# Products of zeros on TensorE, PSUM operands for x and h, and a reordered end in a graph network's layer

## The chip, the cores and the metric

The kernel runs on one core of a Trainium2 chip. The metric is the device time of one execution in microseconds (us), as the median of several runs. A core has five engines that run at the same time and meet through semaphores: TensorE (PE, matrix products, with its weight loads shown apart as PEld), VectorE (DVE), ScalarE (ACT), GpSimd (POOL) and SyncE (SP, which issues most of the DMA transfers). SBUF is the working memory, PSUM the one into which TensorE writes.

## What is computed

12,500 nodes with 128 features each, and 412,500 edges, sorted by target node. In short:

```
h    = relu(layernorm(x)) @ W_in2f                       # 12500 x 128
W_e  = (ssp(edge_attr @ W_f1 + b_f1) @ W_f2 + b_f2) * edge_weight   # 412500 x 128
msg  = h[dst] * W_e
agg  = segment_sum(msg, src, 12500)
out  = x + ssp(agg @ W_o1 + b_o1) @ W_o2 + b_o2          # ssp(v) = softplus(v) - log 2
```

`dst` is sorted, so the rows of `h` that a run of edges reads lie near each other. `src`, over which the messages are summed, is in random order.

## The kernel before

**Chunks.** The edges are taken in 806 chunks (`NCH`) of 512, four tiles of 128 edges each; four chunks make a `Group`. The chunks are split into seven segments (`SEGS`) of 88, 44, 30, 14, 14, 8 and 4 groups. The first ends at chunk 352, the sixth at 792.

**One chunk.** The filter's first layer (`hidden`, L691) is done for two chunks at once, 20 x 512 products into the PSUM tile `z`; ACT takes Abs, Exp and Ln of it (L700 to L703) and DVE puts the softplus together (`hidden_end`, L709). The second layer (`value`, L801) adds four products into a PSUM tile `v` that ACT has filled with the bias (L793). `pick` (L812) chooses the rows of `h` for each edge: DVE marks the place of each edge's target in a window of 32 rows (`at`, L785), and PE multiplies that with the rows, kept as three bf16 parts, into the PSUM tile `picked`; ACT scales them by the edge weight into `hg` (L822). `message` writes `v * hg` into the SBUF tile `o`, of which there are 8 (L829, L830), and POOL scatters `o` with four indirect DMAs (L834) into a table in HBM that has room for several messages of each node. The slot of each message is ranked with two products on PE (`after` and `rest_of`, L733 and L766, into the PSUM tile `free`), and DVE's comparison and maximum (L714, L738). `v` and `picked` share three PSUM buffers. A helper, `behind`, makes some products wait for scatters of some chunks earlier.

**Collecting.** When a segment's messages are in its table, they are loaded back (`load`, L873, into `m`, six buffers), DVE marks which node each belongs to (`compare`, L886, into `to`), and PE sums them per node (`add`, L907, into the PSUM tile `acc`, four blocks of 128 nodes at a time, here called a quad). `keep` then adds `acc` to the running sums `agg` in SBUF (L928 on ACT for the first segment, L930 on DVE for the others). A unit is up to six tiles of one `load`. The units of the first six segments are spread over the steps of later chunks by a small planner. It starts `DELAY` = 7 chunks behind a segment, works out an even rate up to step `NCH + BEYOND`, and then deals the units out to steps; within a step it stops at a unit that ends a quad:

```
        while i < len(todo) and todo[i][0] < k:
            ...
            i += 1
            if todo[i - 1][1].ends(todo[i - 1][2]):
                break
```

**The order.** It is written out by hand (`manual_schedule`): `step(k)` issues, for chunk k, the message; the ends of the ranks before; `keep` of finished quads; for k + 1 the scaling and the second layer; for k + 2 the picking and the bias; then windows, `hidden_end`, the comparison of blocks, `compare` of the step's units, ranks, logarithms, the first layer of a pair four chunks ahead, and `add` of the units (each one unit late). Each engine runs its own part of this in order.

**Making h.** `make_h` does 4 x 128 rows at a time (a quad, 25 in all), one new quad every ninth step: statistics, normalisation, a transpose, Relu, the product `hps` in PSUM, and then three bf16 parts of it. ACT writes the first, DVE subtracts it from `hps` into the SBUF tile `left` (L370), ACT writes the second, DVE subtracts that from `left` for the third (L373).

**The end.** 25 quads of `x` are loaded ahead. The first `NX` = 14 are early ones, from step 300 on, with their bias added by DVE (L426); the others come from step 804 on, into tiles that have come free, with their bias added by POOL. After the last step the last segment is collected, and `finish` applies the output layers to each quad (L436 to L450) and stores it (L453).

Of the kernel before, what the change touches and what calls it, by code (L numbers as in the profile page):

```python
# [17 lines left out]
P = 128  # L18
TG = 16
CH = 512  # L20
# [23 lines left out]
def gnn_kernel(  # L44
# [282 lines left out]
    def make_h(q, psum):  # L327

        n = min(QT, NTILE - q * QT)
        xb = early.pop(q, None)  # L330
        if xb is None:
            xb = load_x(q)
            for _ in range(3):
                yield
        st = ln.tile([P, QT, 6], F32, name="st")
        mv = ln.tile([P, QT, 2], F32, name="mv")
        for i in range(n):
            nc.vector.bn_stats(st[:, i, :], xb[:, i, :])
            nc.vector.bn_aggr(mv[:, i, :], st[:, i, :])

        rs = ln.tile([P, QT], F32, name="rs")
        nc.scalar.activation(rs[:, :n], mv[:, :n, 1], AF.Ln, bias=eps)
        nc.scalar.activation(rs[:, :n], rs[:, :n], AF.Exp, scale=-0.5)
        yield

        ve = ln.tile([P, QT], F32, name="ve")
        nc.vector.tensor_scalar(ve[:, :n], mv[:, :n, 1], EPS, -0.5, op0=ALU.add, op1=ALU.mult)
        r2 = ln.tile([P, QT], F32, name="r2")
        nc.vector.tensor_mul(r2[:, :n], rs[:, :n], rs[:, :n])
        nc.vector.tensor_mul(r2[:, :n], r2[:, :n], ve[:, :n])  # L350
        nc.vector.scalar_tensor_tensor(rs[:, :n], r2[:, :n], 1.5, rs[:, :n],
                                       op0=ALU.add, op1=ALU.mult)
        for i in range(n):
            nc.vector.tensor_scalar(xb[:, i, :], xb[:, i, :], mv[:, i, 0:1], rs[:, i:i + 1],
                                    op0=ALU.subtract, op1=ALU.mult)
        yield
        xps = psum.tile([P, QT, P], F32, name="xps", tag="acc")
        for i in range(n):
            nc.tensor.transpose(xps[:, i, :], xb[:, i, :], ident)
        xT = ln.tile([P, QT, P], F32, name="xT")  # L360
        nc.scalar.activation(xT[:, :n, :], xps[:, :n, :], AF.Relu)
        yield
        hps = psum.tile([P, QT, P], F32, name="hps", tag="acc")
        for i in range(n):
            nc.tensor.matmul(hps[:, i, :], xT[:, i, :], win, start=True, stop=True)
        hb = ln.tile([P, QT, 3, P], BF16, name="hb")
        nc.scalar.activation(hb[:, :n, 0, :], hps[:, :n, :], AF.Copy)
        yield
        left = ln.tile([P, QT, P], F32, name="left")
        nc.vector.tensor_sub(left[:, :n, :], hps[:, :n, :], hb[:, :n, 0, :])  # L370
        nc.scalar.activation(hb[:, :n, 1, :], left[:, :n, :], AF.Copy)
        yield
        nc.vector.tensor_sub(hb[:, :n, 2, :], left[:, :n, :], hb[:, :n, 1, :])  # L373
        for (b, rows), table in zip(tables, h3_t):
            lo = max(0, b - q * QN) // P
            hi = min(n, (b + rows - q * QN) // P)
            if lo < hi:
                r = q * QN + lo * P - b
                nc.sync.dma_start(
                    table[r:r + (hi - lo) * P, :].rearrange("(c p) f -> p c f", p=P),  # L380
                    hb[:, lo:hi, :, :].rearrange("p c k f -> p c (k f)"))
                if b + rows == QN:
                    yield
            if q == NQ - 1:
                for r in range(NTILE * P - b, rows, P):
                    if r >= 0:
                        nc.sync.dma_start(table[r:r + P, :], none)
        nc.sync.dma_start(
            h3[q * QN:q * QN + n * P, :].rearrange("(c p) f -> p c f", p=P),
            hb[:, :n, :, :].rearrange("p c k f -> p c (k f)"))  # L390
        yield
# [28 lines left out]
        for p, cs, rows in pieces:  # L420
            nc.sync.dma_start(xo[:p, cs, :], x[rows, :].rearrange("(c p) f -> p c f", p=p))

    def x_bias(xo, pieces, engine=nc.vector):
        for p, cs, rows in pieces:
            xi = xo[:p, cs, :]
            engine.tensor_add(xi, xi, spread(bo2[:p, :], xi.shape[1]))  # L426

    def finish(t0, n, sT, quad, psum, z, xo=None, bank=("v", 3)):

# [108 lines left out]
    with tc.tile_pool(name="edge", bufs=2) as edge, tc.tile_pool(  # L538
# [8 lines left out]
        free_v = free.rearrange("p (t b) -> p t b", b=NBLK)  # L547


        count_ps = state_ps.tile([P, P], F32, name="count_ps")  # L550

        def clear(seg):

            todo = []

            def put(b, e, low):

                half = seg.tiles(b) * P // 2
                v = seg.views[VIEWS][seg.row(b):seg.row(e), :].rearrange(
                    "(r c) f -> r (c f)", c=half)  # L560
                for q in range(0, 2 * (e - b), P):
                    n = min(P, 2 * (e - b) - q)
                    for r in range(low, half - low, ZN * ZR):
                        w = min(ZN * ZR, half - low - r)
                        todo.append((
                            v[q:q + n, r * RW:(r + w) * RW].rearrange("r (k f) -> r k f", f=ZR * RW),
                            zero[:n, None, :].to_broadcast([n, w // ZR, ZR * RW])))

            full = (NBLK - 1) // BG * BG
            for b, e in ((0, seg.b0), (seg.b0, min(seg.b1, full)), (seg.b1, full)):  # L570
                if b < e:
                    put(b, e, seg.low)

            for b in range(full, NBLK):
                low = seg.low if b < NBLK - 1 else seg.low_last
                half = seg.tiles(b) * P // 2
                n = (half - 2 * low) // ZR
                for r in range(2):
                    r0 = seg.row(b) + r * half + low
                    todo.append((seg.views[VIEWS][r0:r0 + n * ZR, :]  # L580
                                 .rearrange("(q c) f -> q (c f)", c=ZR), zero[:n, :]))
            return todo

        puts = []

# [8 lines left out]
        class Group:  # L594
# [91 lines left out]
            def hidden(self, c):  # L686

                z = psum.tile([P, 2, CH], F32, name="z")
                for k in range(2):
                    rows = slice(32 * (c + k), 32 * (c + k) + RBF)  # L690
                    mm = nc.tensor.matmul(z[:, k, :], wf1[rows, :], self.f[rows, :],  # L691
                                          start=True, stop=True)
                    if k == 0:
                        behind(mm, self.g * NCHUNK + c - LZ, 3)
                self.pair[c] = z
# [110 lines left out]

            def pick(self, c, at, ps):

                near = self.near.pop(c)
                k = self.g * NCHUNK + c - 2  # L810
                for i in range(QT):
                    mm = nc.tensor.matmul(ps[:, i, :], at[:, i * P:(i + 1) * P], near,  # L812
                                          start=i == 0, stop=i == QT - 1, skip_group_check=True)
                    if i == 0:
                        behind(mm, k, 2 + k % 2)
# [118 lines left out]
        groups = {}  # L934
        NEXT = table_of.index(1) - 1
        LG, LW, LR, LZ = 12, 6, 6, 4
        DELAY, BEYOND = 7, 14

        def of(k):
            return groups[k // NCHUNK], k % NCHUNK  # L940
# [52 lines left out]
        def step(k, units=()):  # L993
# [19 lines left out]
                for _ in r:  # L1013
                    pass
            tops.clear()
            for c in owed:
                c.keep()
            owed.clear()
            if has(k + 1):
                g, c = of(k + 1)  # L1020
                hgs[k + 1] = g.picked(c, ps.pop(k + 1))
# [10 lines left out]
            part("blocks", min(k + LR + 1, 2 * k + 3), blocks)  # L1032
            for c, u in units:
                c.compare(u)
            upto = max(made["rank"], min(k + LR, 2 * k + 3))
            ready = [ranks(j) for j in range(made["rank"] + 1, upto + 1)]
            made["rank"] = upto
# [63 lines left out]
                if todo[i - 1][1].ends(todo[i - 1][2]):  # L1101
                    break

        def x_ahead(homes, engine):

            pending = []
            for q, xo in homes:
# [5 lines left out]
                yield  # L1113
                yield
                if len(pending) > 2:
                    x_bias(*pending.pop(0), engine)
            for w in pending:
                yield
                x_bias(*w, engine)

        def as_quad(t):
            return t.rearrange("p (c f) -> p c f", f=P)

        xs = {}
        NX = 14

        def early_homes():
            for q in range(NX):
                if q < 6:
                    yield q, quad.tile([P, QT, P], F32, name="xo", bufs=6)  # L1130
                elif q < 12:
                    yield q, ln.tile([P, QT, P], F32, name="xo", tag=("xb", "xT", "left")[q // 2 - 3],
                                     bufs=2)
                else:
                    t = ln.tile([P, QT, 3, P], BF16, name="xo", tag="hb", bufs=2)
                    yield q, as_quad(t.rearrange("p c k f -> p (c k f)")[:, :2 * CH].bitcast(F32))
# [14 lines left out]
        def rest():  # L1151
# [14 lines left out]
                    yield  # L1166
            yield from ranges(psum)
            late_biases(psum)

        def side():  # L1170

# [11 lines left out]
        with tc.manual_schedule():  # L1183
# [27 lines left out]
            made["rank"] = 0  # L1211
            group(1)
            aside = side()
            x_early = x_ahead(early_homes(), nc.vector)
            x_late = x_ahead(late_homes(), nc.gpsimd)
            for k in range(-3, max(NCH, max(units) + 1)):
                for seg, d in zeros.get(k, ()):
                    seg.clears.append(nc.sync.dma_start(*d).ins.name)
# [122 lines left out]
```

## Time and profile before

| | |
|---|---|
| median of 6 runs | 4225.73 us (4221.04 to 4228.44) |
| profiled execution: time | 4223.44 us |
| profiled execution: span from the first to the last instruction | 4221.6 us |
| busy PE, PEld | 3356.8 us, 2610.9 us |
| busy DVE, ACT, POOL | 3145.7 us, 2775.0 us, 3142.4 us |
| mean granted TensorE clock | 0.828 of full speed |
| moved by DMA | 820.65 MB, 194 GB/s on average |

All rows are of one execution, taken by the hardware profiler. In its lines "L834" is line 834 of the kernel, "slots<-o" the tile written and the one read (POOL's scatter here), "x3224" the number of such instructions; then busy time in us and the mean ns of one, and behind the bar the idle time of the engine just before these instructions with what ended it. Lines of waits give who waited, for whom, the sum in us, how often, and the longest. Lines of the timeline give start, length, engine, line and operation; neighbours alike are merged. A matmul in fp32 is shown as two instructions. The granted clock is what a throttle leaves of TensorE's full speed.

### The profile page before, as it was taken

To read this page: it belongs to the slowest core of one execution; us is meant where nothing else is said; L and a number is where in the kernel's file an instruction comes from. 1 tells how busy PE (TensorE), PEld (TensorE's weight loads), DVE (VectorE), ACT (ScalarE), POOL (GpSimd) and SP (SyncE) were. 2 spreads that over 40 slices of the span, in tenths; PEclk is the share of its full clock that TensorE was granted. 3 is DMA by queue.
4 is the path that set the end of the run, shared out by engine and by line. 5 is a ranking of instruction groups with operands and counts; after the bars stand their busy time and mean duration, and the time that the engine had idled before them with its cause. 6 is when DMAs were issued, how large, how long until landed. Compare 5 with 4: busy or idle time off the path is not lost. (4 is left out here: it accounts for less than half of the span.)

```text
span 4221.6 us, 74340 instructions
## 1 busy us (share of the span) xinstructions
PE 3356.8 (80%) x21594; PEld 2610.9 (62%) x21594; DVE 3145.7 (75%) x7101; ACT 2775.0 (66%) x5466; POOL 3142.4 (74%) x3292
## 2 busy tenths in 40 slices
PE   6777777667767676688888888888888888988888
PEld 4445444444444444467777777776777776777777
DVE  8767666666555555678878877888888888888887
ACT  7767666676666666666666666666666666666644
POOL 6777777777777777777777777777777777777772
PEclk8767666776666766779999899999999998999999
DMA  6665565555444345467777777778777886887776
GB/s 182 199 193 168 165 191 166 156 170 169 140 115 124 110 134 159 141 204 221 223 220 254 232 209 219 212 213 263 227 211 207 260 247 191 231 247 202 206 210 183
DMA packets 515221, 820.65 MB, mean 194 GB/s; under 512 B 177188, under 2 KB 312728, under 8 KB 514812
## 3 DMA queue, kind: packets, MB, share of 16 engines
q1 hardware_dynamic: 411212, 602.55, 50.2%
q0 software_dynamic: 103168, 213.15, 15.0%
q8 instruction: 180, 2.95, 0.3%
q14 instruction: 229, 1.88, 0.2%
q10 hardware_dynamic: 432, 0.13, 0.0%
HBM read 419.75 MB, written 395.69 MB: 193 GB/s over the span
## 5 line engine op out<-in xcount | busy, mean ns | idle before, releaser
L834 POOL DMA_INDIRECT slots<-o,slot x3224 | 3104.9, 963 | 1003.7 <-issue 757.9
L907 PEld LDWEIGHTS acc<-to,m 128*128 128x128 f32 x8152 | 1069.3, 210 | 245.8 <-issue 137.2
L801 PEld LDWEIGHTS v<-wf,r 128*128 128x128 f32 x6448 | 1009.1, 236 | 249.2 <-issue 171.4
L907 PE MATMUL acc<-to,m 128*128 128x128 f32 x8152 | 1133.6, 298 | 28.6 <-DVE to L886 24.0
L822 ACT ACTIVATE hg<-picked,rcut 128x128 f32<-128x128 f32 x3224 | 911.9, 365 | 309.6 <-PE picked L812 224.0
L801 PE MATMUL v<-wf,r 128*128 128x128 f32 x6448 | 1086.6, 323 | 10.3 <-ACT v L793 8.2
L793 ACT ACTIVATE v<-bf 128x512 f32<-128x512 f32 x806 | 484.9, 602 | 694.2 <-DVE o L830 677.5
L691 PE MATMUL z<-f,wf 20*128 20x512 f32 x1612 | 583.7, 807 | 416.5 <-DVE r L709 408.5
L829 DVE COPY o<-place 128x4 f32<-128x4 f32 x806 | 153.5, 190 | 773.5 <-DMA slots<-o,slot 771.9
L886 DVE TENSOR_TENSOR to<-count_ps,m 128x640 f32<-128x640 f32 (+3 forms) x793 | 630.5, 822 | 37.0 <-PE acc L907 31.5
L812 PE MATMUL picked<-near,at 96*128 96x128 bf16 x3224 | 363.0, 243 | 336.6 <-DVE o L830 315.9
L830 DVE TENSOR_TENSOR o<-v,hg 128x512 f32<-128x512 f32 x806 | 552.9, 686 | 58.0 <-PE v L801 50.4
L709 DVE SCALAR_TENSOR_TENSOR r<-z,nbf,a 128x1024 f32<-128x1024 f32 x403 | 512.8, 1273 | 47.1 <-ACT a L703 46.9
L812 PEld LDWEIGHTS <-at 96*128 96x128 bf16 x3224 | 289.4, 111 | 388.6 <-issue 344.0
L700 ACT ACTIVATE a<-z,bf 128x1024 f32<-128x1024 f32 x403 | 443.7, 1101 | 130.7 <-PE z L691 130.5
L691 PEld LDWEIGHTS z<-f,wf 20*128 20x128 f32 x1612 | 146.3, 221 | 600.0 <-DVE r L709 566.0
L703 ACT ACTIVATE a<-a,half 128x1024 f32<-128x1024 f32 x403 | 462.8, 1148 | 13.1
L738 DVE TENSOR_REDUCE top<-free 128x4 f32<-128x392 f32 x806 | 445.9, 553 | 7.6 <-PE free L733 7.6
L714 DVE TENSOR_TENSOR inb<-count_ps,blk 128x392 f16<-128x392 f32 x806 | 443.6, 551 | 0.0
L701 ACT ACTIVATE a<-a 128x1024 f32<-128x1024 f32 x403 | 426.0, 1057 | 12.8
L766 PE MATMUL free<-inb,rest_of 128*128 128x392 f16 x806 | 306.5, 380 | 48.1 <-DVE top L738 33.8
L733 PE MATMUL free<-inb,after 128*128 128x392 f16 x806 | 308.9, 383 | 6.6 <-DVE inb L714 4.1
(113 smaller groups left out, 1358.7 us busy)
## 6 DMA issues: line engine op xcount, KB each, us to landing
m<-slots SPq DMA_DIRECT2D x307, 387.0 KB
m<-slots SPq DMA_DIRECT2D x278, 322.5 KB
rel<-rel_d SPq DMA_DIRECT2D x202, 384.0 KB
slots<-o,slot POOLq DMA_INDIRECT x3224
m<-slots SPq DMA_DIRECT2D x193, 258.0 KB
slots<-zero SPq DMA_DIRECT2D x96, 387.0 KB
f<-in_f_t SPq DMA_DIRECT2D x404, 80.0 KB
slots<-zero SPq DMA_DIRECT2D x58, 516.0 KB
```

The source lines that it names most:

```text
L691: mm = nc.tensor.matmul(z[:, k, :], wf1[rows, :], self.f[rows, :], start=True, stop=True)
L703: nc.scalar.activation(a, a, AF.Ln, bias=half, scale=0.5)
L709: nc.vector.scalar_tensor_tensor(r, z, nbf1, a, op0=ALU.max, op1=ALU.add)
L738: nc.vector.tensor_reduce(self.top[:, c * QT:(c + 1) * QT], free_v, axis=mybir.AxisListType.X, op=ALU.max)
L793: nc.scalar.activation(v, spread(bf12, QT), AF.Copy)
L801: mm = nc.tensor.matmul(v[:, i, :], r[:, i * P:(i + 1) * P], wf2, start=False, stop=True, skip_group_check=True)
L812: mm = nc.tensor.matmul(ps[:, i, :], at[:, i * P:(i + 1) * P], near, start=i == 0, stop=i == QT - 1, skip_group_check=True)
L822: nc.scalar.activation(hg[:, i, :], ps[:, i, :], AF.Copy, scale=self.rcut[:, j:j + 1])
L830: nc.vector.tensor_mul(o[:, :, :P], v, hg)
L834: put = nc.gpsimd.indirect_dma_start(out=views[j % VIEWS], out_offset=bass.IndirectOffsetOnAxis(ap=self.slot[:, j:j + 1], axis=0), in_=o[: ...
L886: nc.vector.tensor_tensor(to[:, :n, :], count_ps[:, None, :].to_broadcast([P, n, P]), m[:, :n, P:].to_broadcast([P, n, P]), op=ALU.is_equal)
L907: nc.tensor.matmul(self.acc[b // QT][:, i, :], m[:, j, :P], to[:, j, :], start=t == 0, stop=t == self.seg.tiles(b) - 1)
```

## The change

Five edits in one diff.

1. `make_h` writes the first difference back into `hps` in PSUM instead of into `left` in SBUF, and the second difference reads it there.
2. The bias of the early `x` quads is read from a copy in PSUM (`bo2_ps`), which shares a bank with `count_ps`. ACT makes the copy once.
3. A new helper, `idle`, multiplies a tile of zeros (`none`) with itself, 384 columns in bf16, into a PSUM tile that the next products overwrite. In front of each picking it is called for 6 products up to chunk 358 and for 4 after that; in front of each first filter layer, of two chunks, for 12 up to chunk 358. The first 8 chunks have none.
4. In steps behind the last chunk `keep` is issued after the first `compare` of the step instead of ahead of it. `BEYOND` goes from 14 to 8.
5. `NX` goes from 14 to 16, with two more buffers for early `x` quads.

```diff
-        left = ln.tile([P, QT, P], F32, name="left")
-        nc.vector.tensor_sub(left[:, :n, :], hps[:, :n, :], hb[:, :n, 0, :])
-        nc.scalar.activation(hb[:, :n, 1, :], left[:, :n, :], AF.Copy)
+        nc.vector.tensor_sub(hps[:, :n, :], hps[:, :n, :], hb[:, :n, 0, :])
+        nc.scalar.activation(hb[:, :n, 1, :], hps[:, :n, :], AF.Copy)
         yield
-        nc.vector.tensor_sub(hb[:, :n, 2, :], left[:, :n, :], hb[:, :n, 1, :])
+        nc.vector.tensor_sub(hb[:, :n, 2, :], hps[:, :n, :], hb[:, :n, 1, :])
...
-    def x_bias(xo, pieces, engine=nc.vector):
+    def x_bias(xo, pieces, engine=nc.vector, b=bo2):
         for p, cs, rows in pieces:
             xi = xo[:p, cs, :]
-            engine.tensor_add(xi, xi, spread(bo2[:p, :], xi.shape[1]))
+            engine.tensor_add(xi, xi, spread(b[:p, :], xi.shape[1]))
...
-        count_ps = state_ps.tile([P, P], F32, name="count_ps")
+        numbers = state_ps.tile([P, CH], F32, name="numbers")
+        count_ps, bo2_ps = numbers[:, :P], numbers[:, P:2 * P]
...
+        def idle(bank, n):
+
+            for _ in range(n):
+                nc.tensor.matmul(bank[:, :3 * P], none[:, :P], none, start=True, stop=True,
+                                 skip_group_check=True)
...
                 z = psum.tile([P, 2, CH], F32, name="z")
+                if 8 <= self.g * NCHUNK + c < segs[1].c0 + DELAY:
+                    idle(z[:, 0, :], 12)
...
             def pick(self, c, at, ps):
 
+                if self.g * NCHUNK + c >= 8:
+                    early = self.g * NCHUNK + c < segs[1].c0 + DELAY
+                    idle(ps.rearrange("p t f -> p (t f)"), 6 if early else 4)
...
-        DELAY, BEYOND = 7, 14
+        DELAY, BEYOND = 7, 8
...
-            for c in owed:
-                c.keep()
-            owed.clear()
+            def keep():
+                for c in owed:
+                    c.keep()
+                owed.clear()
+
+            if k < NCH or not units:
+                keep()
...
             for c, u in units:
                 c.compare(u)
+                keep()
...
-        NX = 14
+        NX = 16
...
+            nc.scalar.activation(bo2_ps, bo2, AF.Copy)
...
-            x_early = x_ahead(early_homes(), nc.vector)
-            x_late = x_ahead(late_homes(), nc.gpsimd)
+            x_early = x_ahead(early_homes(), nc.vector, bo2_ps)
+            x_late = x_ahead(late_homes(), nc.gpsimd, bo2)
```

More of the change, by code (lines that the diff above doesn't have):

```diff
@@ L1102, in gnn_kernel, with x_ahead @@
                     break
-        def x_ahead(homes, engine):
+        def x_ahead(homes, engine, b):
             pending = []
@@ L1115, in x_ahead @@
                 if len(pending) > 2:
-                    x_bias(*pending.pop(0), engine)
+                    x_bias(*pending.pop(0), engine, b)
             for w in pending:
                 yield
-                x_bias(*w, engine)
+                x_bias(*w, engine, b)
         def as_quad(t):
@@ L1124, in gnn_kernel @@
         xs = {}
-        NX = 14
+        NX = 16
         def early_homes():
             for q in range(NX):
[L1129 to L1132, printed above, removed]
+                if q < 8:
+                    yield q, quad.tile([P, QT, P], F32, name="xo", bufs=8)
+                elif q < 14:
+                    yield q, ln.tile([P, QT, P], F32, name="xo", tag=("xb", "xT", "left")[q // 2 - 4],
                                      bufs=2)
```

## The prediction, made before the changed kernel ran

> **What bounds the kernel now.** I read the page first, for the engine with the least room. GpSimd (POOL) is busy 74% of the span, no more than the others, yet its scatters and the wait for them stand out:
>
> ```profile
> L834 POOL DMA_INDIRECT slots<-o,slot x3224 | 3104.9, 963 | 1003.7 <-issue 757.9
> L829 DVE COPY o<-place 128x4 f32<-128x4 f32 x806 | 153.5, 190 | 773.5 <-DMA slots<-o,slot 771.9
> ```
>
> POOL's idle is the 0.3 us in front of nearly every scatter, named "issue": it waits for nobody. The period is 0.958 (median) + 0.305 = 1.263 us, so one chunk of 512 edges (four scatters) takes 5.05 us, and 3224 x 1.263 = 4072 us of the 4088 between the first scatter's start (23.3) and the last one's (4111.6). VectorE (DVE) in turn waits 772 us for a free `o` buffer, that is for POOL. So POOL sets the pace, and only three things can shorten the run: the 16 us by which POOL is over its pace, the 23 us before, the 110 us behind.
>
> Next the stretches, by windows (columns: window, its length, busy time and instructions of PE, PEld, DVE, ACT, POOL; granted clock, DMA share, GB/s):
>
> ```profile
> 400.00:1800.00 1400.00, 976.85 (x4580) 661.74 (x4581) 862.79 (x2165) 940.72 (x1864) 1064.55 (x1101) 0.68 0.51 149
> 1900.00:3860.00 1960.00, 1706.93 (x12712) 1425.76 (x12708) 1616.42 (x3373) 1283.45 (x2532) 1487.22 (x1551) 0.92 0.76 225
> 3860.00:4087.00 227.00, 195.35 (x1514) 167.05 (x1515) 200.54 (x416) 141.11 (x280) 172.20 (x180) 0.94 0.71 203
> 4087.00:4112.00 25.00, 20.12 (x159) 18.25 (x157) 18.14 (x30) 0.00 (x0) 18.90 (x21) 1.00 1.02 305
> 4112.00:4140.00 28.00, 22.94 (x182) 20.84 (x180) 20.74 (x33) 0.00 (x0) 13.89 (x13) 1.00 0.97 283
> ```
>
> Then the waits of DVE in the second of these, and in the third, where POOL is missing from the list:
>
> ```profile
> DVE o L829 <- DMA slots<-o,slot: 197.8, 146, 3.6
> DVE agg L930 <- PE acc L907: 43.2, 35, 4.0
> DVE o L830 <- PE v L801: 37.0, 30, 3.0
> ```
> ```profile
> DVE agg L930 <- PE acc L907: 18.8, 17, 4.0
> ```
>
> 1900 to 3860 is 388 steps of 5.05 us: DVE is busy 4.17 and waits 0.51 for POOL, so it could step in 4.54. From 3860 on it never waits for POOL: those 45 steps are bound by DVE and what it waits for, and the lead of the messages (L830's end to the chunk's first scatter) falls from some 30 us at chunk 720 to 20 at the last. The run then ends with DVE's own chain: last message 4087, late sums to 4140, last segment and output to 4221.
>
> Last, the timeline, for what stretches a scatter, and for the steps behind the last message:
>
> ```profile
> 751.13 0.95 POOL L834 DMA_INDIRECT slots<-o,slot  x1 [0.31 <-DMA slots<-o,slot]
> ...
> 752.39 1.90 POOL L834 DMA_INDIRECT slots<-o,slot  x1 [0.30 <-issue]
> ...
> 752.77 0.68 DVE L373 TENSOR_TENSOR hb<-left,hb 128x512 bf16<-128x512 f32 x1
> ```
> ```profile
> 4108.80 0.69 DVE L930 TENSOR_TENSOR agg<-agg,acc 128x512 f32<-128x512 f32 x1 [0.64 <-PE acc L907]
> ...
> 4109.40 1.28 DVE L886 TENSOR_TENSOR to<-count_ps,m 128x512 f32<-128x512 f32 x2
> 4110.14 1.86 PEld L907 LDWEIGHTS acc<-to,m 128*128 128x128 f32 x16 [0.68 <-DVE to L886]
> 4110.14 2.05 PE L907 MATMUL acc<-to,m 128*128 128x128 f32 x16 [0.49 <-DVE to L886]
> ...
> 4111.34 0.69 DVE L930 TENSOR_TENSOR agg<-agg,acc 128x512 f32<-128x512 f32 x1 [0.65 <-PE acc L907]
> ```
>
> The 1.90 us scatter runs beside L373, which has two SBUF inputs; its neighbour at 751.13 took 0.95.
>
> **PSUM operands for h and x.** Over the trace, the 27 scatters that run beside an L373 are 212 ns over the 958 ns median on average, 5.7 us in sum; the 16 beside an L426 add on DVE, also two SBUF inputs, 258 ns, 4.1 us; the 30 beside an L370, which has the same shape but one input in PSUM, 2 ns. After the change all three read one input from PSUM. I take the whole 9.8 us off POOL's chain; the least is 0 (if being beside them is chance), the most 16 (all of its excess). DVE's own time: L370 has a median of 680 ns, L373 678, so 25 + 16 instructions cost nothing. `hps` is held one or two steps longer in the one `acc` bank, but a new quad starts every ninth step and transposes some six steps later, so nobody is queued behind it. One copy of 128 columns on ACT (0.28 us, L1185's row) is free beside ACT's 34% of idle time.
>
> [...]
>
> **Zeros on TensorE (PE).** New: `idle` matmuls of 384 columns in 16 bits. Nearest rows: L766 and L733, 392 columns in 16 bits, which start 0.17 us apart at full clock (3902.34, 3902.51) and 0.33 apart at half (753.51, 753.84). From chunk 8 to 358 there are 6 in front of each picking and 12 in front of each pair's filter layer: 12 a step, 2.0 us at full clock, 4.0 at half. PE idles 423 us in 277 steps there (1.53 a step), and a clock of 0.68 loses it another 0.32 x 5.05 = 1.6. Behind the inserted products on PE's queue stand the pick and filter matmuls, and for those ACT and then DVE wait; DVE has 491 us of waiting for POOL there, 1.77 a step, and the messages lead by 30 us. With the clock up the 2.0 fit into 3.1, and I take 0. At the start the lead is 6 us at chunk 8 and grows by about 1 us a chunk: enough, 0.
>
> From chunk 359 it is 4 a step: 0.67 us (at half clock 1.3). PE idles 0.65 a step in 1900 to 3860 and loses 0.08 x 5.05 = 0.40 to the clock: 1.05 of room. If all of the 0.67 passed on to DVE, its step would be 4.54 + 0.67 = 5.21, over POOL's 5.05; if half, 4.87. I take half: in steps with a filter layer PE then waits for L709 anyway (165 us in 136 waits), which swallows it. So 0 up to 3860. From there no POOL wait covers it: between 0 and 45 x 0.67 = 30 us. L930's 17 waits are what PE's lateness reaches; half of them in steps without a filter layer give 8 x 0.67 = 5.4, less some 2 for the 6% of clock that is won back: +3.4.
>
> [...] The rows agree that the clock follows PE's busy share (0.68 at 70%, 0.92 at 87%); that products of zeros count as busy no row shows.
>
> **The end.** `BEYOND` 8 changes nothing: the loop that deals out the units stops at each finished quad, so from step 806 it gives one quad a step with either value, the last at 824, and both kernels issue the same `m` loads in the same order. Two of the 11 late x loads become early ones, with their bias on DVE at 0.68 each where it waits for POOL: 0. What moves is `keep`: L930 goes behind the first L886 of the next quad, which can fill DVE's 0.65 us of waiting in each of about 20 steps: at most 13 us. But the DMA engines are at 1.02 and 0.97 there. They move 25 x 305 + 28 x 283 = 15.5 MB; 0.5 MB less, at 305 GB/s, takes 49 us for 53. So -4; the least is 0, a wait for `m` in place of the wait for PE.
>
> **Sum** against the profiled execution (span 4221.6, time 4223.4): -9.8 - 4 + 3.4 = -10.4, so 4213.0; the median stands 2.3 above that execution: 4215.3. A measurement can tell about 0.2%, 8.5 us, so the forecast lies just beyond it.
>
> **Rivals.**
> *The zeros become the bound* (slower). In the late steps the insertion lies between PE's pick and the sums that L930 and L886 wait for. It decides once more than 0.51 of the 0.67 us (76%) reaches DVE. At 85%, 4.54 + 0.57 = 5.11: 0.06 x 447 steps = 27 us, so 4242; with all of it 0.16 x 388 + 30 gives 4215 + 89 = 4304. For it: DVE and PE are both over 82% busy. Against: 0.51 us of waiting for POOL a step. Here too belongs that zeros do not lift the clock: 4.0 us against 1.53 in the first segment, +2.5 x 351 = some 870 us. 0.18.
> *The clock wins the end back* (faster). If PE no longer falls to half clock after 3860, the lead stays at 30 us (-10), and if `m` lands in time the full 13 are had (-9): 4196; half of both, 4205. For it: 19 of 227 us are waits of L930 for PE. Against: DVE is busy 88% there. 0.17.
> *Nothing moves*: the stretch of the scatters has another cause and stays, the DMA engines hold the end, and the 3.4 us come on top: 4226 to 4229. 0.10.
> *The forecast*, 4205 to 4228, the bounds of its two small terms: 0.55, some six tenths of it under 4217.
>
> Faster is 0.33 + 0.17 = 0.50; slower 0.18 and a little of the third rival, 0.20; same the rest, 0.30. For eight in ten, from inside the clock rival, 4198, to the first rival at 88%: 5.13 a step, 0.08 x 447 = 36 us, 4250.
>
> **What would show it.** Right: no scatter over 1.3 us beside h's subtraction or x's bias, and L834's mean near 960 ns; a clock over 0.9 in 400 to 1800 with POOL's pace unchanged at 80 scatters in 100 us; DVE still waiting for `o` in 1900 to 3860, by less than 198 us; L930's waits gone behind the last message, with waits for `m` in their place. Wrong: POOL waiting for `o` in late stretches, messages without a lead, or scatters as long as before.

## The result, and the profile after

The changed kernel takes 4215.6 us (median of 18 runs, 4210.1 to 4219.1), the kernel before, on the same chip and in turn with it, 4226.6 (38 runs): a ratio of 0.9974, interval 0.9968 to 0.9980. That is 11.0 us (8.5 to 13.5) less; forecast were 4215.3 us and 10.4 us. The profiled execution has a span of 4212.8 us against 4221.6.

Eight of the twelve runs told below fell on two other chips, on which the kernel before itself takes 5365 and 5386 us; a ratio is always taken against the kernel before on the same chip.

The lines move by 8 to 11 in the new file: the scatter is L845, the copy and product of a message L840 and L841, the addition of a late sum L941, its comparison L897, the zeros L587. Of the page, the lines of POOL, of DVE's wait for it, and the new ones of PE:

```profile
L845 POOL DMA_INDIRECT slots<-o,slot x3224 | 3093.3, 959 | 1007.4 <-issue 756.3
L587 PE MATMUL picked<-none 128*128 128x384 bf16 x3894 | 776.8, 330 | 155.9 <-DVE o L841 155.1
L840 DVE COPY o<-place 128x4 f32<-128x4 f32 x806 | 153.4, 190 | 642.3 <-DMA slots<-o,slot 641.0
L587 PE MATMUL z<-none 128*128 128x384 bf16 x2112 | 387.1, 335 | 92.0 <-DVE r L717 91.6
```

3224 scatters of 958 ns would be 3088.6 us: what lies over that has fallen from 16.3 to 4.7 us. The 6006 products of zeros keep PE busy for 1164 us. DVE's wait for POOL (the line of L840) falls from 772 to 641 us and is still the largest that DVE has: POOL sets the pace as before.

The windows, with the columns of before:

```profile
400.00:1800.00 1400.00, 1196.67 (x7937) 767.24 (x7936) 868.57 (x2172) 947.10 (x1878) 1062.43 (x1108) 0.98 0.51 151
1900.00:3860.00 1960.00, 1850.72 (x14279) 1502.19 (x14277) 1621.78 (x3380) 1288.68 (x2538) 1486.97 (x1552) 0.97 0.76 226
3860.00:4087.00 227.00, 213.06 (x1654) 175.00 (x1653) 199.44 (x406) 135.12 (x269) 172.38 (x180) 0.97 0.72 202
4087.00:4112.00 25.00, 21.23 (x169) 19.43 (x169) 18.68 (x29) 0.00 (x0) 20.19 (x20) 1.00 1.02 311
4112.00:4140.00 28.00, 24.30 (x189) 21.87 (x188) 22.89 (x37) 3.36 (x6) 4.05 (x5) 1.00 0.87 254
```

In the first stretch the clock goes from 0.68 to 0.98 with 3357 more matmuls, and POOL does 1108 scatters where it did 1101: TensorE's clock is won and nobody needs it. In the second it goes from 0.92 to 0.97, and DVE still waits for POOL, as its waits there show:

```profile
DVE o L840 <- DMA slots<-o,slot: 174.1, 122, 5.5
DVE agg L941 <- PE acc L918: 49.4, 42, 4.0
DVE to L897 <- PE acc L918: 24.6, 36, 2.7
DVE top L746 <- PE free L741: 23.3, 54, 0.9
DVE o L841 <- PE v L809: 22.3, 23, 2.2
```

The waits for PE are 49.4 + 24.6 + 23.3 + 22.3 = 119.6 us; the three of before were 43.2 + 37.0 + 28.5 = 108.7. So 10.9 us in 388 steps, 28 ns of the 670 ns a step that the zeros take, reach DVE, and its wait for POOL shrinks by 24 us. Between 3860 and 4087, where nothing covers DVE, its largest wait is shorter than before (18.8):

```profile
DVE agg L941 <- PE acc L918: 17.1, 19, 4.0
```

Two places of the timeline. First h's subtractions beside scatters:

```profile
751.25 0.96 POOL L845 DMA_INDIRECT slots<-o,slot  x1 [0.30 <-issue]
...
751.62 0.68 DVE L372 TENSOR_TENSOR hb<-hps,hb 128x512 bf16<-128x512 f32 x1
...
752.52 0.96 POOL L845 DMA_INDIRECT slots<-o,slot  x1 [0.30 <-DVE hb L372]
```

Both scatters have their 0.96 us, though L372 begins 0.37 us after the first one, where L373 in the kernel before began 0.38 us after the one that took 1.90. Over the whole trace the 31 scatters beside an L372 are 2 ns over the median on average, the 22 beside an x bias on DVE 0.5 ns. Then the steps behind the last message:

```profile
4107.25 1.47 DVE L897 TENSOR_TENSOR to<-numbers,m 128x512 f32<-128x512 f32 x2 [0.63 <-DMA m<-slots]
...
4108.64 0.68 DVE L941 TENSOR_TENSOR agg<-agg,acc 128x512 f32<-128x512 f32 x1
4109.23 0.69 DVE L897 TENSOR_TENSOR to<-numbers,m 128x512 f32<-128x512 f32 x1
...
4110.62 0.69 DVE L897 TENSOR_TENSOR to<-numbers,m 128x512 f32<-128x512 f32 x1 [0.71 <-DMA m<-slots]
```

L941 no longer has an idle time in front of it; L897 has one instead, and what ends it is the transfer of `m`. The waits of DVE from 4087 to 4145 say it in sums (before: 13.0 us in 20 waits of the addition for PE, 1.1 us for `m`; the middle line belongs to the output):

```profile
DVE to L897 <- DMA m<-slots: 6.4, 11, 1.2
DVE r_out L441 <- ACT a_out L438: 3.8, 3, 2.3
DVE agg L941 <- PE acc L918: 1.7, 3, 0.8
```

### The profile page after: what moved, and what is told of

It reads as the page before. It is cut to its first block, busy times and chain, and to the rows that moved or that the text cites. A ratio compares the mean times of both kernels' runs of the same rounds, so it can differ in the third digit from the quotient of the medians.

```text
span 4212.8 us, 85440 instructions
## 1 busy us (share of the span) xinstructions
PE 3812.7 (91%) x27600; PEld 2838.3 (67%) x27600; DVE 3156.4 (75%) x7103; ACT 2776.5 (66%) x5467; POOL 3128.3 (74%) x3290
## 5 line engine op out<-in xcount | busy, mean ns | idle before, releaser
L845 POOL DMA_INDIRECT slots<-o,slot x3224 | 3093.3, 959 | 1007.4 <-issue 756.3
L918 PEld LDWEIGHTS acc<-to,m 128*128 128x128 f32 x8152 | 1002.9, 199 | 218.2 <-issue 124.3
L918 PE MATMUL acc<-to,m 128*128 128x128 f32 x8152 | 1060.8, 286 | 19.1 <-DVE to L897 14.9
L587 PEld LDWEIGHTS <-none 128*128 128x128 bf16 x6006 | 596.4, 99 | 606.8 <-issue 328.6
L587 PE MATMUL picked<-none 128*128 128x384 bf16 x3894 | 776.8, 330 | 155.9 <-DVE o L841 155.1
L809 PEld LDWEIGHTS v<-wf,r 128*128 128x128 f32 x6448 | 803.0, 194 | 148.2 <-issue 87.8
L809 PE MATMUL v<-wf,r 128*128 128x128 f32 x6448 | 879.8, 280 | 1.2 <-ACT a L708 0.6
L801 ACT ACTIVATE v<-bf 128x512 f32<-128x512 f32 x806 | 485.2, 602 | 495.0 <-DVE o L841 476.4
L897 DVE TENSOR_TENSOR to<-numbers,m 128x640 f32<-128x640 f32 (+3 forms) x793 | 633.0, 823 | 42.6 <-PE acc L918 28.2
L840 DVE COPY o<-place 128x4 f32<-128x4 f32 x806 | 153.4, 190 | 642.3 <-DMA slots<-o,slot 641.0
L841 DVE TENSOR_TENSOR o<-v,hg 128x512 f32<-128x512 f32 x806 | 552.3, 685 | 85.8 <-ACT a L708 32.3
L699 PE MATMUL z<-f,wf 20*128 20x512 f32 x1612 | 468.8, 658 | 87.8 <-DVE r L717 82.5
L711 ACT ACTIVATE a<-a,half 128x1024 f32<-128x1024 f32 x403 | 462.9, 1149 | 13.1
L587 PE MATMUL z<-none 128*128 128x384 bf16 x2112 | 387.1, 335 | 92.0 <-DVE r L717 91.6
L722 DVE TENSOR_TENSOR inb<-numbers,blk 128x392 f16<-128x392 f32 x806 | 443.6, 551 | 0.0
```

The lines of the kernel that those rows point to most:

```text
L587: nc.tensor.matmul(bank[:, :3 * P], none[:, :P], none, start=True, stop=True, skip_group_check=True)
L711: nc.scalar.activation(a, a, AF.Ln, bias=half, scale=0.5)
L801: nc.scalar.activation(v, spread(bf12, QT), AF.Copy)
L809: mm = nc.tensor.matmul(v[:, i, :], r[:, i * P:(i + 1) * P], wf2, start=False, stop=True, skip_group_check=True)
L841: nc.vector.tensor_mul(o[:, :, :P], v, hg)
L845: put = nc.gpsimd.indirect_dma_start(out=views[j % VIEWS], out_offset=bass.IndirectOffsetOnAxis(ap=self.slot[:, j:j + 1], axis=0), in_=o[: ...
```

## The experiments

The theory is the prediction's: shorter scatters move POOL's whole chain, zeros hide behind POOL's pace, the later `keep` trades DVE's wait for PE against one for `m`. Each part was run alone on the kernel before. The versions that have a profile from a chip like that of the result are read with the same marks, in us. The lead of the last message is the time from the end of its product on DVE to its first scatter; the late sums end where `worst` is reduced:

| | before | e5: PSUM | e6: zeros | e7: keep | e8: no zeros | changed |
|---|---|---|---|---|---|---|
| scatters over 3224 x 958 ns | 16.3 | 6.2 | 24.0 | 14.8 | 6.9 | 4.7 |
| last scatter starts | 4111.6 | 4103.7 | 4123.0 | 4113.1 | 4103.6 | 4103.7 |
| lead of the last message | 20.4 | 18.0 | 21.4 | 20.4 | 23.0 | 17.5 |
| last message to end of late sums | 52.3 | 52.2 | 52.2 | 48.1 | 49.2 | 48.5 |
| span | 4221.6 | 4216.0 | 4231.8 | 4218.9 | 4207.8 | 4212.8 |
| median of the runs | 4226.0 | 4216.5 | 4227.7 | 4220.7 | 4211.0 | 4215.6 |

The medians of e5 to e8 stand beside 4225.95 of the kernel before on their chip, the changed kernel's beside 4226.56. The changes given below follow the ratios; the medians alone would give -9.4, +1.8, -5.3 and -14.9 us for e5 to e8, each inside the interval of its ratio.

**PSUM operands alone (e1, e5).** The core of the edit, on the kernel before:

```diff
-        left = ln.tile([P, QT, P], F32, name="left")
-        nc.vector.tensor_sub(left[:, :n, :], hps[:, :n, :], hb[:, :n, 0, :])
-        nc.scalar.activation(hb[:, :n, 1, :], left[:, :n, :], AF.Copy)
+        nc.vector.tensor_sub(hps[:, :n, :], hps[:, :n, :], hb[:, :n, 0, :])
+        nc.scalar.activation(hb[:, :n, 1, :], hps[:, :n, :], AF.Copy)
...
-            engine.tensor_add(xi, xi, spread(bo2[:p, :], xi.shape[1]))
+            engine.tensor_add(xi, xi, spread(b[:p, :], xi.shape[1]))
```

Expected of e1:

> The kernel before with edits 1 and 2 alone: h's differences and the bias of the early x quads read PSUM. Theory of the forecast (a scatter stretches beside a VectorE instruction with two SBUF inputs): 9 to 12 us faster (ratio 0.9972 to 0.9979), the scatters' mean falls from 963 to some 959 ns, none over 1.3 us beside those lines, the end as before (52 us from the last message to the late sums). Rival (the stretch has another cause): the long scatters stay and the time is within 2 us of before. Rival (the gain of the changed kernel comes from the clock or the end): 0 to 3 us faster.

e1 fell on the chip of 5365 us: 5368.4, ratio 1.0003 (0.9983 to 1.0023). POOL's scatters lie 3.9 us over 3224 x 958 ns, but there POOL itself waits, as the waits of e1 show:

```profile
POOL slots L834 <- DVE o L830: 1260.4, 398, 19.8
```

Half of e1's messages are ready at most 0.28 us before their scatter, where the median lead in the kernel before on the other chip is 30.9 us. With POOL waiting for DVE, the shorter scatters gained nothing there. This says nothing on the 11 us; e5 is the same kernel on a chip like that of the result. Expected of e5:

> The PSUM operands of h and x alone on the kernel before, as in e1. That run fell on a chip where the kernel before takes 5365 us instead of 4226 and where a message is ready only 1 us before its scatter, so that a shorter scatter could not show. Theory (PSUM operands free GpSimd): where the kernel before takes about 4226 us, the scatters' time over the median falls from 16 to about 5 us, the last scatter comes 8 to 11 us earlier and the ratio is 0.9975 (-10 us). Rival (the late sums hold the end, an earlier message is paid back by a longer wait for m): last scatter 8 to 11 us earlier, ratio 0.999. Rival (being beside the subtraction is chance): ratio 1.000, stretch 16 us. Where the kernel before takes 5365 us again: 1.000 by all.

Measured: 4216.5 us, ratio 0.9981 (0.9972 to 0.9990), so -8.0 us (-11.8 to -4.2). The scatters fall from 16.3 to 6.2 us over their median, the last one starts 7.9 us earlier. Of the 10.1 us, 0.5 are lost by a first scatter that starts later (23.8 for 23.3), the other 1.7 between scatters of the first 60 us. The theory stands, by the profile and the time. What is left of the excess is mostly another instruction's: of e5's 105 scatters that are stretched by more than 20 ns, 69 lie beside L785, which marks the places `at` from `rel` in SBUF (4.6 of the 6.2 us, as in the kernel before). In the changed kernel it is 58 of 88, with 3.6 of the 4.7 us.

**Is it the operands? A dose of them (e9, e10).** On the changed kernel without its zeros, 168 additions whose result nobody reads, in every second step, with both inputs in SBUF (e9) or one of them in PSUM (e10); `count_ps` holds a copy of `places`:

```diff
+        dose_t = state.tile([P, QT, 120], BF16, name="dose_t")
...
+            if 16 <= k < 352 and k % 2 == 0:
+                nc.vector.tensor_add(dose_t, spread(places, QT)[:, :, :120], spread(places, QT)[:, :, :120])
```

In e10 the last argument is `spread(count_ps, QT)[:, :, :120]`.

> The changed kernel without its zeros (e8, 4211 us) with 168 more additions on VectorE, one in every second step from 16 to 350, 128x480, both inputs in SBUF; nobody reads their result. VectorE waits 1.77 us a step for o there, so 0.65 us every second step is covered. Theory (a scatter stretches by 212 to 258 ns beside an instruction with two SBUF inputs, 27 scatters for 25 such instructions in the profile before): 168 x 1.08 x 0.212 to 0.258 = 38 to 47 us over e8, 4249 to 4258, and the scatters' time over the median up by as much. Rival (the stretch belongs to h's and x's steps and not to the operands): 4211, stretch as in e8.

> As e9_dose_sbuf, with one of the two inputs of the 168 additions in PSUM (the copy of the same numbers) and nothing else changed. Theory (one input in PSUM leaves GpSimd alone): 4211, stretch as in e8. Rival (VectorE's work stretches scatters wherever it reads): as e9, 4249 or more.

Both fell on the chip of 5386 us, where POOL waits for messages: 5365.1 (0.9960, 0.9941 to 0.9979) and 5395.1 (1.0018, 0.9997 to 1.0040). These times answer nothing about the dose, since e9 has the longer scatters and the shorter time; the difference of the two has no cause that I can show. The scatters themselves can be read. Of each page, POOL's line, of e9 and then of e10:

```profile
L841 POOL DMA_INDIRECT slots<-o,slot x3224 | 3114.3, 966 | 2117.2 <-DVE o L837 1233.4
```
```profile
L841 POOL DMA_INDIRECT slots<-o,slot x3224 | 3090.1, 958 | 2154.6 <-DVE o L837 1273.9
```

25.7 and 1.5 us over 3224 x 958 ns. 204 scatters lie beside an addition of e9 and are 18.4 us over their median in sum; 211 lie beside one of e10 and are 0.07 us over. The two kernels differ in the second input's place alone, so the rival is out. The size was missed: 90 ns a scatter, where 212 to 258 were expected. The timeline of e9 shows why:

```profile
422.16 0.65 DVE L1020 TENSOR_TENSOR dose_t<-places 128x480 bf16<-128x480 f32 x1
422.26 1.39 POOL L841 DMA_INDIRECT slots<-o,slot  x1 [0.30 <-issue]
...
435.06 0.64 DVE L1020 TENSOR_TENSOR dose_t<-places 128x480 bf16<-128x480 f32 x1
...
435.60 0.96 POOL L841 DMA_INDIRECT slots<-o,slot  x1 [0.30 <-issue]
```

The first scatter starts inside an addition that runs on for another 0.55 us, and takes 0.43 us too long. The second starts with 0.10 us of the addition left, and takes its 0.96. Over the trace 103 scatters are stretched by more than 20 ns by an addition, and the addition's end less the scatter's start less the stretch is 126 ns in the median (123 to 131 from the tenth to the ninetieth percentile). In the kernel before, the 22 that L373 and L426 stretch by more than 20 ns give 126 too. So each of these scatters lost the time from 0.126 us after its start to the end of the VectorE instruction. An instruction that began later mostly did no harm: of the 88 scatters of e9 that had started over 0.1 us before the addition, one was stretched (114 ns, which does not fit this addition's end). In the kernel before, eight scatters were stretched by an L373 or L426 that began after them, by 0.11 to 0.20 us in seven cases and by 0.39 us in the prediction's own case at 752.39; others that began from 0.13 us on did nothing. What decides between these is not shown. So the cost of this dose came from where its instructions fell in POOL's period, and in e9 many fell harmlessly: 103 of the 204 scatters beside an addition were stretched by more than 20 ns. In e10 an addition that covers the start left the scatter as it is:

```profile
403.01 0.65 DVE L1020 TENSOR_TENSOR dose_t<-places,numbers 128x480 bf16<-128x480 f32 x1
403.37 0.96 POOL L841 DMA_INDIRECT slots<-o,slot  x1 [5.39 <-DVE o L837]
```

**Zeros alone (e2, e6), and twice as many late ones (e11).** On the kernel before:

```diff
+                if 8 <= self.g * NCHUNK + c < segs[1].c0 + DELAY:
+                    idle(z[:, 0, :], 12)
...
+                if self.g * NCHUNK + c >= 8:
+                    early = self.g * NCHUNK + c < segs[1].c0 + DELAY
+                    idle(ps.rearrange("p t f -> p (t f)"), 6 if early else 4)
```

> The kernel before with edit 3 alone: the products of zeros, as many as in the changed kernel. Theory of the forecast: the granted clock goes to 0.97 or so, GpSimd's pace of 1.263 us does not change, and the time is 0 to 6 us longer (3.4 forecast, from the steps behind 3860 us that no wait for GpSimd covers). Rival (the clock wins the end back): 5 to 10 us faster, with a lead of the messages of some 30 us at the last chunk in place of 20. Rival (the zeros become the bound): 15 us or more slower, and GpSimd waits for VectorE in late stretches.

e2 took 5526.6 us on the chip of 5365: 1.0315 (1.0283 to 1.0346). With no lead of messages and no POOL to hide behind, the zeros cost 161.6 us, 27 ns for each of the 6006. DVE waits 1088 us for PE in e2, and 721 and 768 us in e1 and e3, which have no zeros: the slower rival's mechanism, on a chip where its condition holds. Expected of e6:

> The products of zeros alone, as in e2, where they cost 160 us on the chip on which messages have no lead. Theory (hidden behind GpSimd's pace, a little lead lost at the end): where the kernel before takes about 4226 us, clock 0.97, VectorE still waits over 150 us for o between 1900 and 3860, ratio 1.0000 to 1.0010 (0 to +4 us). Rival (zeros become the bound): ratio 1.004 to 1.02, messages without lead late in the run. Rival (the clock wins the end back): 0.995 to 0.998, lead at the last message 25 us instead of 20. Where the kernel before takes 5365 us again: 1.03 by all.

Measured: 4227.7 us, 1.0004 (0.9995 to 1.0013), so +1.7 us (-2.1 to +5.5). The clock is 0.96 between 400 and 1800 and 0.97 between 1900 and 3860; DVE waits 187 us for `o` there. Neither the slower nor the faster rival: the lead of the last message is 21.4 us for 20.4. The profiled execution, the longest of e6's eleven, is 10 us longer than the one of before, and POOL's chain up to the last scatter is 11.4 us longer. Of these, 7.7 lie in the scatters (24.0 us over 3224 x 958 ns for 16.3) and the rest between scatters of the first 60 us. The subtractions and x biases are not the reason, since the scatters beside them carry 8.3 us for 9.9. All scatters are a little longer: their median is 962 ns for 958. It is 962 in e2, e3 and e4 as well, with and without zeros, so this is not put down to the zeros; its cause stays open.

For e11 the changed kernel has `6 if early else 8` in the line above.

> The changed kernel with 8 products of zeros in front of each late picking instead of 4, 0.67 us more of TensorE a step. The changed kernel leaves VectorE 174 us of waiting for o in 388 steps, 0.45 a step, and the last message a lead of 17.5 us. Forecast's term (half of it reaches VectorE): 0.34 a step is hidden up to 3860, then 45 x 0.34 = 15 us of lead are lost, 4231. If nothing of it reaches VectorE, as e6 and e8 suggest for the first 4: 4216 to 4220. Slower rival (all of it): 0.22 x 388 + 30 = 115 us, 4330.

It too fell on the chip of 5386 us: 5641.0, 1.0451 (1.0414 to 1.0488). There it agrees with e2 (more zeros, more time), but it cannot say from which number on zeros cost time where POOL sets the pace. That point stays open.

**The later keep alone (e3, e7).** On the kernel before:

```diff
-            for c in owed:
-                c.keep()
-            owed.clear()
+            def keep():
+                for c in owed:
+                    c.keep()
+                owed.clear()
+
+            if k < NCH or not units:
+                keep()
...
                 c.compare(u)
+                keep()
```

> The kernel before with the reordered keep alone (NX and BEYOND as before). Theory of the forecast (the DMA engines bound the steps behind the last message): 2 to 5 us faster, waits for m in place of the waits of the running sums for TensorE. Rival (VectorE's order bounded them): 10 to 13 us faster and hardly a wait for m. Rival (nothing, the wait only changes its name): within 1 us.

e3: 5358.6 us on the chip of 5365, 0.9991 (0.9971 to 1.0011). Its late sums end 49.0 us after the last message, where e1 and e2, on the same chip but in the old order, take 55.9 and 58.1.

> The later keep alone, as in e3, where the time from the last message to the last late sum was 49 us against 56 to 58 in the two kernels of that call without it, and the ratio 0.9991. Theory (DMA holds the last sums, 4 us won): where the kernel before takes about 4226 us, 48.5 us in place of 52.3, ratio 0.9991. Rival (all of VectorE's waits for PE are won): 40 us, ratio 0.997. Rival (nothing): 52 us, ratio 1.000.

e7: 4220.7 us, 0.9986 (0.9977 to 0.9995), so -5.9 us (-9.7 to -2.1). The profile has 48.1 us for 52.3, and DVE's waits in it have turned as in the changed kernel:

```profile
DVE to L886 <- DMA m<-slots: 6.2, 12, 1.0
DVE agg L930 <- PE acc L907: 2.1, 6, 0.8
```

**Do the DMA engines hold the late sums? (e12).** The changed kernel without its zeros, with the late loads of x issued in the last segment's steps, behind the late sums:

```diff
-                if k >= NCH - 2:
-                    next(x_late, None)
...
+            late = list(late_homes())
+            x_late = x_ahead(late, nc.gpsimd, bo2)
...
                     stages(q)
                     q += 1
+                    next(x_late, None)
```

> The changed kernel without its zeros (e8, 4211 us), with the loads of the last 9 groups of x issued behind the late sums, one every second step of the last segment, and their bias on GpSimd there, in place of loads between the last scatters. The loads move 2.1 MB out of the 15.5 MB of the late sums. Theory (the DMA engines hold the late sums): 2.1 MB at 305 GB/s is 7 us, of which VectorE's 7.3 us of waiting for m can give up to 6: last message to last late sum 43 us instead of 49, time 4205. Rival (the sums are held by VectorE's own chain or by when m is asked for): 48 to 49 us, 4211. Rival (the tail pays it back, GpSimd's compares wait behind the biases or SyncE's queue is late): 43 us, but 88 instead of 82 behind it, 4211.

5387.7 us on the chip of 5386: 1.0004 (0.9984 to 1.0024). In the stretch of the late sums of e12 the DMA share is 0.78, where e4 (below), the same kernel with the loads in their old place and also on a chip of the slower kind, has 0.95; first e12, then e4:

```profile
5254.00:5306.00 52.00, 45.78 (x340) 43.26 (x339) 37.99 (x60) 0.00 (x0) 5.45 (x6) 0.86 0.78 224
```
```profile
5252.00:5300.00 48.00, 43.46 (x341) 40.07 (x339) 38.60 (x60) 0.00 (x0) 14.88 (x14) 0.98 0.95 280
```

Yet the sums end 52.4 us after the last message in e12 and 48.2 in e4, with 3.5 and 4.9 us of DVE's waits for `m`. Taking 2.1 MB out won nothing there; but PE ran at 0.86 of its clock in e12 and DVE waited for it (9.1 us, in e4 4.0), so the run does not say what it would be where PE keeps up. On the chip of e12 itself, e9 and e10, with the late steps of e4, take 51.2 and 49.5 us: a microsecond or two is the spread of this mark there. Behind the sums it takes 81.7 us as ever: the moved loads cost the tail nothing. That the DMA engines hold the late sums is argued from the share of 1.02 and the waits for `m`, not shown.

**Everything but the zeros (e4, e8).** The changed kernel without the two insertions and `idle`.

> The changed kernel without its products of zeros. Theory of the forecast: faster than the changed kernel by 0 to 6 us, so 11 to 16 us faster than before (ratio 0.9962 to 0.9974), at the old clock of some 0.83. Rival (the clock is part of the gain): slower than the changed kernel, 5 us or more of the gain lost.

e4: 5365.1 us, 0.9996 (0.9977 to 1.0015), on the chip of 5365, where e1's shorter scatters had gained nothing either (1.0003); its late sums take 48.2 us, as in e3 (49.0).

> The changed kernel without its products of zeros, as in e4. Theory (PSUM -10, end -4, zeros +3): where the kernel before takes about 4226 us, ratio 0.9967 (-14 us), 3 us under the changed kernel, lead of the last message 20 us or more, last message to last late sum 48 us. Rival (the zeros help through the clock): ratio 0.998 to 0.999, above the changed kernel's 0.9974. Rival (parts don't add, the DMA engines hold the end): as the changed kernel, 0.9974. Where the kernel before takes 5365 us again: 1.000 by all.

e8: 4211.0 us, 0.9969 (0.9957 to 0.9981), so -13.1 us. It is the fastest version run, 2 us under the changed kernel by the ratios, but the two intervals overlap: that it beats the changed kernel is not shown where POOL sets the pace. On the slower chip of e2, zeros alone cost 3%; the changed kernel itself was not run on such a chip. Of the versions here it is the one that I would keep.

## Why the prediction was right

**The sum.** The three parts alone give -8.0, +1.7 and -5.9, together -12.2, against -9.8, +3.4 and -4 in the prediction; the changed kernel has -11.0. Within their intervals the parts add up, and every term of the prediction lies inside its part's interval. These intervals are some 4 us wide to either side, so the mechanisms are confirmed, but that the total came within 1 us of the forecast is partly luck: the gain from the scatters was smaller than its term at the last scatter, and the zeros cost less than theirs if anything.

**PSUM operands, -9.8.** The step was that the excess beside L373 and L426 goes and moves POOL's whole chain. It went: 10.1 us in e5, 11.6 in the changed kernel. The last scatter comes 7.9 us earlier in both, not 10, since 2 to 4 us came back as idle time of POOL in the first 60 us, which the term left out. The forecast took "beside" as the condition and a mean of 212 and 258 ns as the price; e9 shows that it matters what VectorE does early in the scatter, from 0.126 us after its start, and that the mean is a matter of phase.

**PSUM operands cost DVE next to nothing.** L370 and L373 took 682 and 678 ns, their successors L369 and L372 take 693 and 679, and the additions of e10 and e9, alike but for the place of one input, 643 and 647.

**Zeros, 0 up to 3860 and +3.4 behind it.** The start was put at 0 on a lead of 6 us at chunk 8. With zeros the lead there is 2.4 and 2.5 us (e6, changed kernel) for 5.8 to 7.0 without, and 9 for 20 us at chunk 20: the zeros do reach DVE there, though POOL no longer waits. In the first 100 us POOL's idle time before scatters, over its usual 0.305 us each, is 6.1 and 4.9 us with zeros and 1.6, 3.2, 4.5 and 2.4 without (before, e5, e7, e8), so a cost of a few us at the start is possible and not shown. From 60 us to 3860 they stayed hidden, as forecast. That they would raise the clock was the author's estimate: the kernel before had 0.68 with PE busy 70% and 0.92 with 87%, and no products of zeros. It went to 0.98 (0.96 in e6) from 400 to 1800, and behind 3860 from 0.94 to 0.97 (0.98 in e6), so 3 to 4 of the 6% that the term took as won back came. The step "half of the 0.67 us reaches DVE" was mis-sized: between 1900 and 3860 it is 28 ns a step of 670, 4%. In the last 45 steps DVE's largest wait for PE is 17.1 and 15.4 us with zeros (changed kernel, e6) and 18.8, 24.4, 21.0 and 19.1 without (before, e5, e7, e8), so there PE is if anything earlier with them, as the clock rival had it. What this gives the lead can't be told: it is 1.0 us longer in e6 than before, and 5.5 us shorter in the changed kernel than in e8. The measured +1.7 (-2.1 to +5.5) allows the 3.4, and allows 0 as well.

**The end, -4.** 52.3 to 48.1 in e7, 52.2 to 49.2 from e5 to e8, 52.2 to 48.5 from e6 to the changed kernel: 3 to 4.2 us, as worked out from the bytes, with the waits for `m` in the place of those for PE. That the bytes are the reason is left open by e12.

**Nothing else moved.** `BEYOND` changes nothing, as forecast: with 14 instead of 8 the changed kernel has the same instructions in the same order on every engine. Two more early loads of x are in e8 and not in e5 and e7; 13.1 against 8.0 + 5.9 leaves nothing to see of them.

**The rivals.** The slower one needed over 0.51 us a step to reach DVE where POOL sets the pace; 0.028 did. On the chip of e2, where POOL does not set it, its mechanism holds, and zeros alone made the kernel 3.15% slower. The prediction named the condition (a POOL that DVE waits for), and had no row from which it could have seen that some chips do not meet it. The clock rival wanted a lead of 30 us at the last message; the changed kernel has 17.5. That nothing moves is ruled out by e5, e7 and the pair e9 and e10.

## What to carry to other kernels

Where GpSimd's indirect DMAs set the pace, look at what VectorE runs as each of them starts: here an addition or subtraction with two SBUF inputs that was running 0.126 us after the scatter's start stopped it until it ended (103 scatters in e9, 22 in the kernel before), and the same addition with one input in PSUM did not (0.07 us over 211 scatters of e10), at the same speed (647 and 643 ns). The marking of `at` (L785) is what is left of such scatters (58 of 88 in the changed kernel). Work that is put in to hide behind an engine's pace, as the zeros were, cost nothing that shows while that engine was the bound (e6: +1.7 us, -2.1 to +5.5) and 161.6 us where it was not (e2): measure on more than one chip, or leave out what buys no time where it is free. Parts run alone, and read by the same three or four marks of the trace, told more here than the total.

## What the hardware showed unexpectedly

**A scatter is stopped, not slowed.** The 958 ns scatter gets on for 126 ns and loses the time from there to the end of the VectorE instruction (103 cases in e9, 22 in the kernel before). The additions with both inputs in SBUF stretched scatters by 18.4 us in sum (e9), those with one input in PSUM by 0.07 (e10). Which of the two began first did not settle it: eight scatters of the kernel before were stopped by an instruction that began 0.11 to 0.39 us after them, while in e9 the additions that began over 0.1 us after a scatter left it alone in 87 of 88 cases.

**Products of zeros kept the clock up.** 12 of them a step took the granted clock between 400 and 1800 from 0.68 to 0.98 (0.96 in e6, the zeros alone; 0.68 in e8, everything but the zeros), although POOL's pace, and so the rate of all other work, stayed the same (1108 scatters there for 1101).

**The same kernel takes 27% longer on one chip than on another, with instructions of VectorE, ScalarE and GpSimd as short.** On the slower chips the median scatter still takes 958 to 962 ns; in e1 the product of a message on DVE (L830) takes 685 ns for 686 in the kernel before, ACT's Abs (L700) 1104 for 1101. TensorE's products are longer (L801 342 ns for 323). The granted clock is lower there (0.754 in e1, 0.825 in e5), but e2 has 0.879 and takes longer still. SyncE's register, assert and move instructions took over 0.3 us in 485 of 3228 cases in e1, and in none of 3228 in the kernel before and the changed one; TensorE, VectorE and ScalarE were idle together for over 2 us 103 times (369 us) in e1 and 9 times (22 us) before. What held them up there is not shown.
